# Local transformer in a chain of blocks: the mask into the scores' banks by ScalarE, the state transposed once and spread through DRAM, a step's scores ahead of its weighted state

## The chip, the cores and the metric

The kernel runs on one core of one Trainium2 chip. Its engines work side by side, each through its own queue in order: TensorE (PE, with the weight loads as PEld), VectorE (DVE), ScalarE (ACT), GpSimd (POOL), and SyncE (SP), which issues the DMAs. They wait for each other through semaphores. The metric is device microseconds of one execution; several executions are made and their median is taken.

## The reference

Two blocks follow each other, each an attention and a feed-forward part with modulated layer norms, on x of 16 batch rows, 256 positions, 128 channels. What the change touches is the second part of the first block, a local transformer of 6 layers:

```
for i in range(6):
    x = attn_layer(shift_tokens(x), Wqkv[i], q_scale[i], k_scale[i], Wo[i]) + x
    x = ffn_layer(shift_tokens(x), ...) + x

def attn_layer(x, Wqkv, qs, ksc, Wo):         # 16 heads of 64
    q, k, v = heads of x @ Wqkv
    q = l2norm(q) * qs;  k = l2norm(k) * ksc
    q = q * cos * scale + rotate_half(q) * sin * scale
    k = k * cos / scale + rotate_half(k) * sin / scale
    # windows of 32 queries, each on 64 keys: its own window and the one before
    sim = q_window @ k_two_windows.T * 8
    sim = where(mask, -max, sim)              # i < j or i > j + 32 or no key
    out = softmax(sim) @ v_two_windows
    return out @ Wo
```

Everything is float32.

## The kernel before, in words

The local transformer keeps its state in eight SBUF tiles `zs[u]`, one for each unit u of two batch rows, channels on the partitions, with 32 columns of zeros ahead of the 256 positions (PAD), so that a window's 64 keys are 64 neighbouring columns. The values are not projected: the weights of value and output are merged once a layer (`merge_vo`), so that a head's output is its weighted state (probabilities times the state's rows) times a merged matrix.

One loop (L1050) runs over 192 steps: 6 layers x 8 units x 4 steps, where a step handles two pairs of heads of one unit. It is a pipeline written out by hand: pass n of the loop issues, in this order, work of several steps:

- `scaled` (L792, L795): POOL multiplies the keys of step n-4 by their inverse norms, which come spread over the partitions in tiles `kn`; two pairs, so two instructions.
- `merging` (L924, L927): PE multiplies the weighted state of step n-9 by the merged matrices into the bank `y`.
- parts of earlier units' feed-forward (`ffn`, L948), handed out piece by piece by `go_on`.
- `rotate` (L712, L714): POOL adds the rotated halves `got` to queries and keys of step n-1, four instructions.
- `flipped` (L884, L888): PE turns the probabilities of step n-5, in two halves, into `prT`.
- `windows` (L797): twice in four steps, for one batch row each, PE transposes eight windows of 64 columns of the state (L805), DVE and ACT copy them to `xw`, and a DMA copies partitions 0 to 63 of `xw` to 64 to 127 (L813), so that the two heads of a pair find the rows on their own half of the array.
- `masked` (L816, L821): PE writes the mask into the two banks of the scores by an identity matmul, from a bf16 tile; the scores are then accumulated on it.
- `norms_sum` (L717) in even passes: PE sums squares of two steps.
- `weighted` (L898, L906): for step n-8, two rounds of eight matmuls, each round into two banks, which ACT (L921) and DVE (L919) copy to `zx`.
- `scores` (L832, L843): 128 small matmuls for step n-4, half of them on the keys of each pair, into two banks; then `maxima` (L852) on DVE: a maximum (L855) and its scaled negative `nb` (L857) for each bank.
- `norms_inverse` (L734) in even passes, and parts of `ffn`.
- `project` (L685) of step n, for two pairs of heads: each time two products of weights and state on PE (L698), and for each the square on ACT (L701) and two products with rotary tables on DVE (L703 into `sent`, L706 into q or k). Four DMAs then exchange halves of `sent` into `got` (L708, L709). Ahead of each square stands a quarter of `exponentials` (L860, L865) of the first pair of step n-4: two ACT instructions of 64 columns.
- the rest: `divided` (L876: a reciprocal on DVE, L878, and a product on POOL, L880) of the first pair, the exponentials of the second pair, and its `divided`.
- `widened` (L781, L786): four DMAs that spread the inverse norms of step n-3 from DRAM into two tiles `kn`.

On PE, DVE, ACT and POOL this program order is the order of the queues. The order of SP's DMAs is made by the scheduling layer. PSUM has eight banks here: four that rotate for all products (`bank()`, L58), three for scores (`sim`), one for `y`. The temporaries of `work` rotate through eleven buffers of 128x512, `kn`, `got` and `sent` through two each.

Of the kernel before, what the change touches and what calls it, by code (L numbers as in the profile page):

```python
# [10 lines left out]
F32 = mybir.dt.float32  # L11
# [7 lines left out]
B, L, D = 16, 256, 128  # L19
NU = B // 2  # L20
# [24 lines left out]
def adaln_kernel(  # L45
# [12 lines left out]
    def bank():  # L58
        return stage["ps"].tile([128, 512], F32, tag="mm", name="mm")
# [20 lines left out]
    def small(tag, shape, bufs=4):  # L80
        return (stage.get("small") or sm).tile(list(shape), F32, tag=tag, name=tag, bufs=bufs)
# [518 lines left out]
    with ExitStack() as es:  # L600
# [23 lines left out]
        nc.sync.dma_start(sel, io["c_sel"])  # L624

        ks = [persistent(f"k{j}", (128, 2, PAD + L)) for j in range(8)]
        rope = lc.tile([128, 2, 2, L], F32, tag="rope", name="rope")
        nc.sync.dma_start(rope, io["c_rope"].rearrange("p (j a) t -> p j a t", j=2))

# [164 lines left out]
            k = ks[m % 8][:, :, PAD:]  # L794
            nc.gpsimd.tensor_tensor(k, k, two(kn), ALU.mult)  # L795

        def windows(u, s):  # L797


            xw = atile("xw", (128, 8, 128))  # L800
            for g in range(2):
                pt = bank()
                for j in range(4):
                    w0 = 32 * (4 * g + j)
                    nc.tensor.transpose(  # L805
                        pt[0:64, j * 128 : (j + 1) * 128], zs[u][:, s, w0 : w0 + 64], ident
                    )
                dst = xw[0:64, 4 * g : 4 * g + 4, :].rearrange("p w d -> p (w d)")
                if g:
                    nc.vector.tensor_copy(dst, pt[0:64, :])  # L810
                else:
                    nc.scalar.copy(dst, pt[0:64, :])
            nc.sync.dma_start(xw[64:128], xw[0:64])  # L813
            return xw

        def masked():  # L816

            sims = []
            for par in range(2):
                sim = pss.tile([128, 512], F32, tag="sim", name="sim")  # L820
                nc.tensor.matmul(  # L821
                    sim,
                    ident16,
                    maskb.unsqueeze(1).to_broadcast([128, 2, 256]),
                    start=True,
                    stop=False,
                    skip_group_check=True,
                )
                sims.append(sim)
            return sims  # L830

        def scores(sims, m, qs):  # L832

# [42 lines left out]
        def divided(pr, ssum):  # L876
            rsum = small("rsum", (128, 8))
            nc.vector.reciprocal(rsum, ssum.rearrange("p t h -> p (t h)"))  # L878
            prf = pr.rearrange("p t h k -> p (t h) k")
            nc.gpsimd.tensor_tensor(  # L880
                prf, prf, rsum.unsqueeze(2).to_broadcast([128, 8, 64]), ALU.mult
            )

        def flipped(p, x, pr, prT):  # L884

            pt = bank()
            for st in range(4):
                nc.tensor.transpose(  # L888
                    pt[:, st * 128 : (st + 1) * 128],
                    pr[:, x, st].rearrange("p h k -> p (h k)"),  # L890
                    ident,
                )
            if x:
                nc.vector.tensor_copy(prT[:, p + x, :], pt)
            else:
                nc.scalar.copy(prT[:, p + x, :], pt)

        def weighted(j, xw, prT):  # L898

            zx = atile("zx", (128, 2, NP, 128))  # L900
            for k in (2 * j, 2 * j + 1):
                pz = [bank(), bank()]
                for w in range(2):
                    for par in range(2):
                        r = slice(64 * par, 64 * par + 64)
                        nc.tensor.matmul(  # L906
                            pz[par][:, w * 256 : (w + 1) * 256],
                            xw[r, (2 * k + w) % 8, :],
                            prT[r, :, 64 * k + 32 * w : 64 * k + 32 * w + 32],
                            start=True,  # L910
                            stop=True,
                            skip_group_check=True,
                        )
                for par in range(2):
                    c0 = 64 * (k % 2)
                    dst = zx[:, par, :, c0 : c0 + 64].rearrange("p a (w q) -> p w a q", w=2)
                    src = pz[par].rearrange("p (w a q) -> p w a q", w=2, a=NP)
                    if par:
                        nc.vector.tensor_copy(dst, src)  # L919
                    else:  # L920
                        nc.scalar.copy(dst, src)  # L921
            return zx

        def merging(j, zx, vo, py):  # L924
# [125 lines left out]
        while n < N + 9 or behind:  # L1050
# [26 lines left out]
            for s, lag in ((0, 7), (1, 9)):  # L1077
                v, r = divmod(n - lag, QS)
                if r == 0 and 0 <= v < DEPTH * NU:
                    xws[v, s] = windows(v % NU, s)  # L1080
            sims = masked() if 0 <= n - 4 < N else None
            if 0 <= n - 5 < N:
                flipped(p, 1, prs.pop(n - 5), prTs[i, u])

            if n % 2 == 0 and 2 <= n <= N:
                n2 = norms_sum([squares.pop(m) for m in range(2 * n - 4, 2 * n)])
            v, r = divmod(n - 8, QS)
            if 0 <= v < DEPTH * NU:
# [32 lines left out]
            if layer + 1 < DEPTH:  # L1121
# [476 lines left out]
```

## Time and profile before

| | us |
|---|---|
| median of three runs | 4208.1 (4206.4 to 4209.5) |
| the profiled execution, its own time | 4207.8 |
| its span, first to last instruction | 4206.0 |
| the layer loop, by the rows of its scores (L843) | about 303 to 3572 |
| a unit of four steps, 2006.49 to 2074.08 | 67.59 |

Mean granted clock of TensorE over the span: 0.981. In the layer loop each step's rows repeat with small differences, so that one unit of four steps, read engine by engine, tells most of the loop. In the profile's rows the first numbers are a start and a length in us, or, in groups, the busy time and the mean length in ns of one instruction and then the idle time ahead of them and what ended it. "SPq" is the queue of DMA issues. The shares of the span are averages: which wait ends last is read from the rows of a step.

### The profile page before, as it was taken

Reading aid. Unit: us, or ns where it says so; the run is one execution under the profiler, and the core shown is the slowest. Engines: PE = TensorE matmul, PEld = TensorE weight load, DVE = VectorE, ACT = ScalarE, POOL = GpSimd, SP = SyncE. Lnnn points to the kernel's source line nnn. Section 1 sums busy time; section 2 is a strip of 40 time slices with the busy share of each in tenths; the row PEclk is TensorE's granted clock in tenths of the full one; section 3 lists DMA queues with packets and bytes.
Section 4 is the critical chain, followed back from the end, with each engine's and each line's share of the span. In section 5 each row is a group of like instructions: output and inputs, shape, how many; then the busy total and the mean of one; then the engine's idle time right before and its main releaser. Section 6 shows DMA issues by size and latency. Waiting matters only on the chain.

```text
span 4206.0 us, 118202 instructions
## 1 busy us (share of the span) xinstructions
PE 3938.9 (94%) x45491; PEld 2580.1 (61%) x45491; DVE 2856.0 (68%) x6005; ACT 2753.1 (65%) x9640; POOL 2655.1 (63%) x3374
## 2 busy tenths in 40 slices
PE   7877999999999999999999999999999999799998
PEld 4534666666666666666666666666666666455554
DVE  6746767677767767676777777776767675476664
ACT  4535666667666666667666667666666766276665
POOL 5446666776666676666676766767666665155453
PEclk9878999999999999999999999999999999899999
DMA  1333444444444444444444444444434442200000
GB/s 41 41 90 97 106 109 105 109 107 105 106 105 114 104 110 105 105 110 102 111 109 105 112 103 106 108 110 105 110 100 105 104 105 72 64 1 6 9 3 11
DMA packets 193547, 371.06 MB, mean 88 GB/s; under 512 B 42537, under 2 KB 83416, under 8 KB 192984
## 3 DMA queue, kind: packets, MB, share of 16 engines
q1 hardware_dynamic: 192984, 363.50, 34.3%
q8 instruction: 360, 5.90, 0.6%
q14 instruction: 203, 1.66, 0.1%
HBM read 127.92 MB, written 8.91 MB: 33 GB/s over the span
## 4 chain that ended last, share of the span: by engine, by line
PE 46%; DVE 22%; ACT 19%; issue 7%; POOL 5%; DMA 1%; SPq 0%; POOLq 0%; DVEq 0%; ACTq 0%
ACT pr L865 11%; PE mm L906 9%; PE sim L843 7%; DVE sent L703 6%; ACT sq L701 4%; PE mm L722 4%; PE mm L888 4%; POOL pr L880 4%; DVE k L706 3%; DVE q L706 3%; PE mm L698 3%; DVE mx L855 3%; PE mm L805 2%; PE mm L1376 2%; PE sim L1303 2%
## 5 line engine op out<-in xcount | busy, mean ns | idle before, releaser
L865 ACT ACTIVATE pr<-sim,nb,rq 128x64 f32<-128x64 f32 x3072 | 1229.5, 454 | 336.8 <-DVE nb L857 318.3
L880 POOL TENSOR_TENSOR pr<-pr,rsum 128x512 f32<-128x512 f32 x384 | 398.3, 1042 | 807.3 <-DVE rsum L878 761.8
L865 ACT ACTIVATION_READ_ACCUMULATOR pr<-sim,nb,rq 128x1 f32 x3072 | 784.5, 255 | 0.0
L927 PEld LDWEIGHTS y<-zx,wvo 128*128 128x128 f32 x6144 | 716.1, 192 | 92.1 <-issue 89.0
L927 PE MATMUL y<-zx,wvo 128*128 128x128 f32 x6144 | 717.7, 275 | 1.3 <-ACT zx L921 1.2
L698 PE MATMUL mm<-z,wqk 128*128 128x512 f32 x1536 | 706.9, 602 | 8.6 <-DMA wqk<-in_L_ffn_Wqkv_dram 6.7
L703 DVE SCALAR_TENSOR_TENSOR sent<-mm,vec,rope 128x512 f32<-128x512 f32 x768 | 570.4, 743 | 118.2 <-ACT sq L701 110.2
L714 POOL TENSOR_TENSOR q<-q,got 128x512 f32<-128x512 f32 x384 | 488.3, 1272 | 12.7 <-DMA got<-sent 10.2
L714 POOL TENSOR_TENSOR k<-k,got 128x512 f32<-128x512 f32 x384 | 496.2, 1292 | 0.0
L795 POOL TENSOR_TENSOR k<-k,kn 128x512 f32<-128x512 f32 x384 | 481.9, 1274 | 17.9 <-DMA kn<-rkh 17.9
L701 ACT ACTIVATE sq<-mm 128x512 f32<-128x512 f32 x768 | 475.7, 619 | 23.3 <-PE mm L698 23.3
L698 PEld LDWEIGHTS mm<-z,wqk 128*128 128x128 f32 x1536 | 278.7, 192 | 322.9 <-issue 234.7
L919 DVE COPY zx<-mm 128x512 f32<-128x512 f32 x384 | 265.6, 692 | 262.0 <-PE mm L906 262.0
L921 ACT COPY zx<-mm 128x512 f32<-128x512 f32 x384 | 224.9, 586 | 287.0 <-PE mm L906 287.0
L906 PE MATMUL mm<-prT,xw 64*128 64x256 f32 x3072 | 389.7, 391 | 3.8 <-DVE zx L919 2.0
L855 DVE TENSOR_REDUCE mx<-sim 128x8 f32<-128x512 f32 x384 | 263.1, 685 | 171.9 <-PE sim L843 171.9
L906 PEld LDWEIGHTS mm<-prT,xw 64*128 64x128 f32 x3072 | 293.5, 187 | 121.7 <-issue 92.2
L1346 POOL TENSOR_TENSOR pr<-pr,rsum 128x256 f32<-128x256 f32 (+1 forms) x256 | 205.1, 832 | 241.7 <-DVE rsum L1344 218.3
L888 PE MATMUL mm<-ident,pr 128*128 128x128 f32 x1536 | 244.6, 282 | 105.1 <-POOL pr L880 75.9
L888 PEld LDWEIGHTS mm<-ident,pr 128*128 128x128 f32 x1536 | 174.9, 142 | 270.0 <-POOL pr L880 240.6
L843 PEld LDWEIGHTS sim<-k,q 64*32 64x32 f32 x24576 | 265.8, 105 | 83.3 <-issue 55.2
L843 PE MATMUL sim<-k,q 64*32 64x64 f32 x24576 | 299.7, 226 | 15.9 <-POOL k L795 8.1
(253 smaller groups left out, 6461.5 us busy)
## 6 DMA issues: line engine op xcount, KB each, us to landing
got<-sent SPq DMA_DIRECT2D x1536, 128.0 KB
kn<-rkh SPq DMA_DIRECT2D x768, 128.0 KB
xw<-xw SPq DMA_DIRECT2D x96, 256.0 KB
wqk<-in_L_ffn_Wqkv_dram SPq DMA_DIRECT2D x48, 128.0 KB
bhome<-brow SPq DMA_DIRECT2D x1, 3072.0 KB
wv<-in_L_ffn_Wqkv_dram SPq DMA_DIRECT2D x12, 256.0 KB
wo<-in_L_ffn_Wo_dram SPq DMA_DIRECT2D x12, 256.0 KB
xt<-in_x_dram SPq DMA_DIRECT2D x8, 256.0 KB
```

The source lines that it names most:

```text
L698: nc.tensor.matmul(pp, wqk[:, j, :], xs, start=True, stop=True)
L701: nc.scalar.activation(sq, pp, AF.Square)
L703: nc.vector.scalar_tensor_tensor(two(sent[:, j, :]), two(pp), scale, tab[1], ALU.mult, ALU.mult)
L714: nc.gpsimd.tensor_tensor(r, r, two(got[:, j, :]), ALU.add)
L795: nc.gpsimd.tensor_tensor(k, k, two(kn), ALU.mult)
L843: nc.tensor.matmul(sims[par][32 * c : 32 * c + 32, c0 : c0 + 64], q[r, s, t0 : t0 + 32], k[r, s, t0 : t0 + 64], start=False, stop=True, sk ...
L855: nc.vector.tensor_reduce(mx, sim.rearrange("p (b k) -> p b k", b=8), AX.X, ALU.max)
L865: nc.scalar.activation(pr[:, x, st, par, :], sims[par][:, b * 64 : (b + 1) * 64], AF.Exp, bias=nbs[par][:, b : b + 1], scale=rn[:, par, b ...
L880: nc.gpsimd.tensor_tensor(prf, prf, rsum.unsqueeze(2).to_broadcast([128, 8, 64]), ALU.mult)
L888: nc.tensor.transpose(pt[:, st * 128 : (st + 1) * 128], pr[:, x, st].rearrange("p h k -> p (h k)"), ident,)
L906: nc.tensor.matmul(pz[par][:, w * 256 : (w + 1) * 256], xw[r, (2 * k + w) % 8, :], prT[r, :, 64 * k + 32 * w : 64 * k + 32 * w + 32], star ...
L927: nc.tensor.matmul(py[:, j * 128 : (j + 1) * 128], vo[:, h, :], zx[:, h % 2, h // 2, :], start=(h == 0), stop=(h == 2 * NP - 1), skip_grou ...
```

## The change

There are four edits, all in the local transformer.

1. The state is transposed once a unit (`upright`, new): four transposes of 128 columns into one bank, one ACT copy to `xt`, two DMAs that store it row by row into a DRAM tile `rows` (two of them, used in turn, each with 32 zero rows ahead). `windows` then no longer uses PE, DVE or ACT: four DMAs load 32 partitions each of `xw` from the DRAM rows, for either half.
2. `masked` fills one bank a call instead of two, and is called twice a pass, for the step after the one whose scores are made in this pass: once behind `flipped`, once at the end. After the first three banks it is an ACT copy from the bf16 mask to the bank; the first three are still matmuls.
3. `scores` and `maxima` of step n-4 stand ahead of `weighted` of step n-8.
4. Exponentials and division are one sequence (`softmax`): its first quarter is issued between the two rounds of `weighted`, the next ones ahead of the squares of `project` (so the first pair's division comes ahead of the last square), the rest at the end.

```diff
+        rows = [dr.tile([2, PAD + L, D], F32, tag=f"rows{j}", name=f"rows{j}") for j in range(2)]
...
-        def windows(u, s):
+        def upright(u, home):
+
+            pt = bank()
+            for t in range(4):
+                s, c = t // 2, PAD + 128 * (t % 2)
+                nc.tensor.transpose(
+                    pt[:, t * 128 : (t + 1) * 128], zs[u][:, s, c : c + 128], ident
+                )
+            xt = work("xt").rearrange("p (s h d) -> p s h d", s=2, h=2)
+            nc.scalar.copy(xt.rearrange("p s h d -> p (s h d)"), pt)
+            for s in range(2):
+                nc.sync.dma_start(
+                    home[s, PAD : PAD + L, :].rearrange("(h p) d -> p h d", p=128), xt[:, s]
+                )
+
+        def windows(s, home):
             xw = atile("xw", (128, 8, 128))
...
-            nc.sync.dma_start(xw[64:128], xw[0:64])
+            for r in range(0, 128, WIN):
+                t0 = r % (2 * WIN)
+                nc.sync.dma_start(
+                    xw[r : r + WIN],
+                    home[s, t0 : t0 + L, :].rearrange("(w p) d -> p w d", p=WIN),
+                )
             return xw
+        banks = []
         def masked():
...
+            if len(banks) < 3:
+                nc.tensor.matmul(
+                    sim, ident16, src, start=True, stop=False, skip_group_check=True
+                )
+            else:
+                nc.scalar.copy(sim.rearrange("p (x c) -> p x c", x=2), src)
+            banks.append(sim)
...
+        def softmax(*args):
+
+            for x in range(2):
+                yield from exponentials(x, *args)
+                pr, ssum = args[-2:]
+                divided(pr[:, x], ssum[:, x])
...
-        def weighted(j, xw, prT):
+        def weighted(j, xw, prT, between):
...
+                if k % 2 == 0:
+                    next(between, None)
             return zx
...
-                    xws[v, s] = windows(v % NU, s)
-            sims = masked() if 0 <= n - 4 < N else None
+                    if s == 0:
+                        upright(v % NU, rows[v % 2])
+                    xws[v, s] = windows(s, rows[v % 2])
             if 0 <= n - 5 < N:
                 flipped(p, 1, prs.pop(n - 5), prTs[i, u])
+            if 0 <= n - 3 < N:
+                masked()
+            sims = banks[2 * (n - 4) : 2 * (n - 3)] if 0 <= n - 4 < N else None
...
-            v, r = divmod(n - 8, QS)
-            if 0 <= v < DEPTH * NU:
-                zxs[v, r] = weighted(r, xws[v, r // 2], prTs[v // NU, v % NU])
-            go_on(behind)
             if sims:
...
                 nbs = [maxima(sims[par], rn[:, par]) for par in range(2)]
                 ssum = small("ssum", (128, 2, 4, 2))
+                between = softmax(sims, nbs, rn, pr, ssum)
+            else:
+                between = iter(())
+            v, r = divmod(n - 8, QS)
+            if 0 <= v < DEPTH * NU:
+                zxs[v, r] = weighted(r, xws[v, r // 2], prTs[v // NU, v % NU], between)
+            go_on(behind)
...
-            between = exponentials(0, sims, nbs, rn, pr, ssum) if sims else iter(())
...
             if sims:
-                for x in range(2):
-                    for _ in between:
-                        pass
-                    divided(pr[:, x], ssum[:, x])
-                    between = exponentials(1, sims, nbs, rn, pr, ssum) if x == 0 else iter(())
+                for _ in between:
+                    pass
                 prs[n - 4] = pr
             if 0 <= n - 3 < N:
+                masked()
```

More of the change, by code (lines that the diff above doesn't have):

```diff
@@ L626, in adaln_kernel @@
         ks = [persistent(f"k{j}", (128, 2, PAD + L)) for j in range(8)]
+        rows = [dr.tile([2, PAD + L, D], F32, tag=f"rows{j}", name=f"rows{j}") for j in range(2)]
+        zero = work("zero")[0:PAD, 0:D]
+        nc.vector.memset(zero, 0.0)
+        for home in rows:
+            for s in range(2):
+                nc.sync.dma_start(home[s, 0:PAD, :], zero)
         rope = lc.tile([128, 2, 2, L], F32, tag="rope", name="rope")
@@ L795, in scaled @@
             nc.gpsimd.tensor_tensor(k, k, two(kn), ALU.mult)
-        def windows(u, s):
-            xw = atile("xw", (128, 8, 128))
[L801 to L812, printed above, removed]
-            nc.sync.dma_start(xw[64:128], xw[0:64])
+        def upright(u, home):
[7 more added lines that the diff above has]
+            nc.scalar.copy(xt.rearrange("p s h d -> p (s h d)"), pt)
+            for s in range(2):
+                nc.sync.dma_start(
+                    home[s, PAD : PAD + L, :].rearrange("(h p) d -> p h d", p=128), xt[:, s]
+                )
@@ L814, in windows @@
+        def windows(s, home):
+            xw = atile("xw", (128, 8, 128))
+            for r in range(0, 128, WIN):
[4 more added lines that the diff above has]
+                )
             return xw
+        banks = []
         def masked():
-            sims = []
-            for par in range(2):
-                sim = pss.tile([128, 512], F32, tag="sim", name="sim")
+            sim = pss.tile([128, 512], F32, tag="sim", name="sim")
+            src = maskb.unsqueeze(1).to_broadcast([128, 2, 256])
+            if len(banks) < 3:
@@ L821, in masked @@
                 nc.tensor.matmul(
[L822 to L827, printed above, removed]
-                )
-                sims.append(sim)
-            return sims
+                    sim, ident16, src, start=True, stop=False, skip_group_check=True
+                )
+            else:
+                nc.scalar.copy(sim.rearrange("p (x c) -> p x c", x=2), src)
```

## The prediction

> **What bounds the kernel now.** The sum is made against the profiled execution, 4207.8 us: a span of 4206.0 and 1.8 around it. The median of the three runs, 4208.1, is 0.3 away. I read the page first (busy shares, chain), then the stretches between two blocks of scores, then one step engine by engine, then the places where a load came late.
>
> ```profile
> PE 3938.9 (94%) x45491; PEld 2580.1 (61%) x45491; DVE 2856.0 (68%) x6005; ACT 2753.1 (65%) x9640; POOL 2655.1 (63%) x3374
> ...
> PE 46%; DVE 22%; ACT 19%; issue 7%; POOL 5%; DMA 1%; SPq 0%; POOLq 0%; DVEq 0%; ACTq 0%
> ```
>
> TensorE (PE) is nearly always busy, but only 46% of the chain lies on it. The layer loop has 192 steps, four to a unit. The stretches of one unit, cut where a block of scores (L843) ends (columns: length, then busy PE, PEld, DVE, ACT, POOL, then clock):
>
> ```profile
> 2006.49:2023.27 16.78, 16.55 (x218) 10.60 (x218) 12.75 (x21) 10.58 (x40) 10.35 (x9) 1.00 0.43 114
> 2023.27:2039.26 15.99, 15.21 (x219) 11.81 (x219) 11.57 (x22) 11.01 (x42) 11.50 (x22) 1.00 0.42 102
> 2039.26:2056.65 17.39, 17.13 (x222) 10.60 (x222) 11.16 (x19) 13.58 (x44) 12.98 (x11) 1.00 0.41 107
> 2056.65:2074.08 17.43, 16.66 (x215) 11.14 (x214) 12.76 (x23) 11.88 (x42) 12.25 (x22) 1.00 0.41 99
> ```
>
> I call them I to IV: 67.59 us a unit, 48 units. The end of I, by the timelines of PE, POOL and the DMA queue:
>
> ```profile
> 2017.38 0.66 PE L888 MATMUL mm<-ident,pr 128*128 128x128 f32 x4 [0.23 <-POOL pr L880]
> 2017.97 1.92 PE L722 MATMUL mm<-sq,sel 128*32 128x512 f32 x16
> 2019.86 2.00 PE L906 MATMUL mm<-prT,xw 64*128 64x256 f32 x16
> 2021.79 1.48 PE L843 MATMUL sim<-k,q 64*32 64x64 f32 x128
> ```
> ```profile
> 2016.29 1.04 POOL L880 TENSOR_TENSOR pr<-pr,rsum 128x512 f32<-128x512 f32 x1 [0.47 <-DVE rsum L878]
> 2017.29 2.52 POOL L795 TENSOR_TENSOR k<-k,kn 128x512 f32<-128x512 f32 x2
> ```
> ```profile
> 2015.72 0.59 SPq L709 DMA_DIRECT2D got<-sent  x1
> 2018.59 2.41 SPq L786 DMA_DIRECT2D kn<-rkh  x4
> ```
>
> PE waits only for the division (L880). POOL's two scalings of k (L795) end at 2019.81, and the scores need them at 2021.79, because the weighted state (L906) stands between: 2 us of slack. The kn loads go out after the eight got loads, and 13 to 17 us ahead of the scaling that uses them. A third thing is seen on DVE, beside POOL's row (third line):
>
> ```profile
> 2006.52 0.69 DVE L855 TENSOR_REDUCE mx<-sim 128x8 f32<-128x512 f32 x1 [0.78 <-PE sim L843]
> 2007.24 0.37 DVE L857 SCALAR_TENSOR_TENSOR nb<-mx,rq 128x8 f32<-128x8 f32 x1
> ```
> ```profile
> 2006.33 1.25 POOL L714 TENSOR_TENSOR q<-q,got 128x512 f32<-128x512 f32 x1
> ```
>
> The small nb row takes 0.17 alone, but here it ends 0.03 after POOL's row does: it sits out POOL's instruction. Last, one of the six steps where a kn load stood behind the got loads:
>
> ```profile
> 2219.09 0.59 SPq L709 DMA_DIRECT2D got<-sent  x1
> 2219.73 5.51 SPq L786 DMA_DIRECT2D kn<-rkh  x5
> ```
> ```profile
> 2220.10 1.30 POOL L795 TENSOR_TENSOR k<-k,kn 128x512 f32<-128x512 f32 x1
> 2222.75 1.28 POOL L795 TENSOR_TENSOR k<-k,kn 128x512 f32<-128x512 f32 x1 [1.35 <-DMA kn<-rkh]
> ```
>
> The scaling starts 3.0 us after the issue (2.9 to 3.8 over the six) and POOL stands 1.35 us; the slack hides it, that step took 16.9.
>
> **The change part by part.** *Taken from PE.* The two mask matmuls move PE on by 0.43 us (2016.55 at full pace; the next starts at 2034.77 + 0.43 in II). The sixteen transposes of a unit cost 0.87 and 1.03, the four that replace them as much as a flip, 0.45. That is 4 x 0.43 + 1.90 - 0.45 = 3.2 us a unit. The waits of PE for the division sum to 1.8 a unit. Alone: -5.0 x 48 = -240.
>
> *Masks on ScalarE.* Two copies of 128x512; no row writes a bank from SBUF. Bounds: 0.24 (L776, the smallest copy) and 0.59 (L921); 0.59, as it has that shape. One stands behind the step's last exponential, while reciprocal, division and scaling run (0.2 + 1.04 + 2.5); the other while PE sums norms. Cost 0; without cover 1.18 x 192 = 226.
>
> *Spread through DRAM.* Ten DMAs for two a unit, at 0.6 issue each. The first load waits for the stores: at most 3.8 us twice by the late loads above, plus 3.6 issue, against a whole step until it is used. Cost 0 on PE. DMA share 0.42 leaves room for the bytes, +0.75 MB on 7 a unit.
>
> *Scores ahead of the weighted state.* Clock: T is the end of a block of scores. Scalings now stand directly before the scores' second half (0.85 to T), and POOL's four rotations follow until T+4.27, with borders at T+0.43, 1.71, 2.99. DVE does maxima first: mx to 0.72, nb to 1.73 (border), mx to 2.44, nb to 3.02, and only then its zx copies, to 3.73 and 4.42; before, they stood ahead of the maxima. PE takes banks from a ring of four, and the second bank wanted after the weighted state (1.96 long) is the one this first copy empties. So PE waits at T+3.8: I, project's second product, 0.95; II, the state's mean (L953), 1.4; III, project's first, 1.7 (POOL has L972 and L974 ahead of the rotations, borders 0.4 later); IV, project's first, 1.4. PE's path: I 16.78 - 0.43 - 0.40 + 0.95 = 16.9. III 17.39 - 0.35 - 0.65 + 1.7 = 18.1. IV 17.43 less masks, windows and waits (2.4), + 1.4 = 16.4.
>
> ACT's chain: zx copies (0.48 pace) and two pairs of exponentials (0.77) stand before the first square. In II that square waits for the product behind the late mean: T+5.65, before T+2.37. From there to the last exponential it was 7.98; one pair is done already: 12.9. Reciprocal and division to 14.3, scalings to 16.85, scores: **II 17.65**. IV, with its table load (1.28) now between copy and exponentials: last exponential 11.9, division 13.25, scaling 15.8, **16.6**.
>
> *What the DMA queue does.* SP's own order moves too. As the changed program is built, in the steps before even ones (those that end I and III) 184 of the 192 loads of the second kn tile stand behind the eight got loads, before 10; of the first tile 46, before 2. In order on one queue, they wait for got, and got for the fourth `sent` of project. I: first square T+3.9, `sent` rows from 4.55 at 0.66 each, with a reciprocal: fourth ends 9.5; four got issues to 12.0; kn at 12.0, 12.55, 13.15; plus 3.0: scalings 15.0 and 16.3 to 17.55; + 0.85: **I 18.4** (PE's 16.9 is shorter). III: L980 and L981 on DVE (0.68 + 0.85) come before `sent`: fourth ends 11.25, got 13.75, kn 14.3, landed 17.3, scaled 18.6: **III 19.45**. The slack that hid this is gone, since scores no longer stand behind the weighted state.
>
> Sum: 18.4 + 17.65 + 19.45 + 16.6 = 72.1, +4.5 a unit, x 48 = +216: 4207.8 + 216 = 4424. Ends from the kn delay (2.9 to 3.8): 4414 to 4500 (two steps x 0.8 x 48).
>
> [...] The clock: with PE's waits in II and III there may be dips. The trace shows one behind waits of 2.02 and 1.84 us near the loop's end:
>
> ```profile
> 3582.70:3589.50 6.80, 6.04 (x20) 4.38 (x21) 2.12 (x4) 1.17 (x2) 0.00 (x0) 0.50 0.01 2
> ```
>
> In it the weighted state took 3.88 for 2.00. One such dip a unit costs at most half of 6.8: +163. [...]
>
> **The rivals.** *A: kn lands in time after all* (0.20). Then I is 16.9 and III 18.1, the bank wait and ACT's chain alone decide: 69.25, +80: 4288. For it: before, kn needed 3 us of a lead of 13 to 17. Against: the order as built.
>
> *B: faster* (0.14). If DVE's copy doesn't hold PE's bank (the nb rows don't meet POOL, as in 102 of 339 in the trace) and kn is in time, the first square of II isn't late: I 16.0, II 15.5, III 16.4, IV 16.4: 64.3, -158: 4050. It decides where the kn wait at POOL stays under 0.5 us and the bank wait under 0.3.
>
> *C: dips* (0.13): 4424 + 163 = 4587. For it: with 86% busy (65.5 less the 3.2 taken, of 72.1), PE is between the loop's 97% at clock 1.00 and its tail.
>
> *D: no change* (0.03), where A's loss meets B's gain.
>
> **How the numbers follow.** Forecast 0.50: 4424. Below it A and B, above it C. The range from 4220 to 4600 leaves out B and part of D; below A's 4288 I go by half the bank waits (5.45 x 48 / 2 is 131, of which about half lies on the path, so 4288 - 66). The forecast's own range is 4340 to 4510. A measurement of this kernel can tell about 0.2% from no change. Faster 0.15 (B and a part of D), same 0.03, slower 0.82.
>
> **What would show it.** Right: in the groups, POOL's scaling of k idle for DMA kn, in all 200 us or more (before 17.9); scores idle for POOL k; PE or PEld of project and mean idle for the DVE zx copy; stretches of about 18, 18, 19, 17; no mask and fewer transposes on PE. Wrong: if POOL's scaling still waits 20 us in all, I and III are too long here; if project doesn't wait for zx, II and IV too. What would make it wrong at the root: `sent` early enough that got and kn go out sooner, or nb that doesn't wait for POOL.

## The result, and the profile after

The changed kernel takes 4391 us at the median (4386 to 4394), the kernel before 4208: the ratio is 1.043, with a 95% interval from 1.042 to 1.045. That is 183 us more; the forecast was 216 more. The profiled execution has a span of 4389.3 us.

The page of the changed kernel, busy shares and chain:

```profile
PE 3884.4 (88%) x44534; PEld 2548.8 (58%) x44534; DVE 2870.8 (65%) x5910; ACT 2900.3 (66%) x9973; POOL 2655.2 (60%) x3374
...
PE 27%; DVE 23%; issue 11%; POOL 11%; ACT 10%; DMA 9%; SPq 8%; POOLq 0%; DVEq 0%; ACTq 0%
```

TensorE (PE) was busy 3939 us before and is busy 3884 now, and its share of the chain fell from 46% to 27%. What is new on the chain is DMA (9%, before 1%) and SP's queue (8%, before 0%). One unit of four steps, cut at the ends of the scores (columns as in the forecast: length, busy PE, PEld, DVE, ACT, POOL, clock):

```profile
1955.83:1974.12 18.29, 16.80 (x216) 10.56 (x215) 12.97 (x21) 11.46 (x42) 9.54 (x9) 1.00 0.60 150
1974.12:1991.53 17.41, 14.48 (x209) 10.77 (x209) 11.27 (x21) 11.46 (x43) 13.23 (x22) 1.00 0.46 114
1991.53:2010.56 19.03, 16.92 (x220) 10.68 (x220) 11.95 (x19) 14.59 (x46) 11.06 (x11) 1.00 0.36 96
2010.56:2027.03 16.47, 15.43 (x210) 10.82 (x209) 12.58 (x22) 12.72 (x44) 13.24 (x22) 1.00 0.38 91
```

PE's work in the unit came down from 65.55 to 63.63 us, and the unit got longer, 71.2 for 67.6. Over the units of the loop, its first and last ones left out, the medians of I to IV are 18.96, 17.73, 18.96 and 16.48 (forecast 18.4, 17.65, 19.45, 16.6).

The end of I, first SP's queue, then POOL:

```profile
1962.30 0.53 SPq L715 DMA_DIRECT2D got<-sent  x1
...
1966.81 0.59 SPq L716 DMA_DIRECT2D got<-sent  x1
1967.44 1.88 SPq L793 DMA_DIRECT2D kn<-rkh  x3
```
```profile
1966.54 1.04 POOL L895 TENSOR_TENSOR pr<-pr,rsum 128x512 f32<-128x512 f32 x1 [1.02 <-DMA got<-sent]
1970.38 1.27 POOL L802 TENSOR_TENSOR k<-k,kn 128x512 f32<-128x512 f32 x1 [2.79 <-DMA kn<-rkh]
```

Three of the four kn loads go out at 1967.44, behind the last got load. The scaling starts 2.9 us later, and POOL stood 2.79 us for it. In the kernel before, the scaling came 14 us behind its last load's issue at the median. In all, the groups of POOL's scaling, PE's projection, and the mask copies read:

```profile
L705 PE MATMUL mm<-z,wqk 128*128 128x512 f32 x1536 | 721.7, 609 | 95.9 <-DVE zx L941 87.0 <-DMA wqk<-in_L_ffn_Wqkv_dram 7.7 <-ACT wvT L678 0.7
...
L802 POOL TENSOR_TENSOR k<-k,kn 128x512 f32<-128x512 f32 x384 | 484.3, 1272 | 298.3 <-DMA kn<-rkh 288.9 <-DMA xw<-rows 6.3 <-DMA wqk<-in_L_ffn_Wqkv_dram 1.1
...
L844 ACT CAST sim<-maskb 128x512 f32<-128x512 bf16 x381 | 245.4, 644 | 0.0
```

and POOL's scaling in the kernel before:

```profile
L795 POOL TENSOR_TENSOR k<-k,kn 128x512 f32<-128x512 f32 x384 | 481.9, 1274 | 17.9 <-DMA kn<-rkh 17.9
```

POOL's wait for kn is 288.9 us in all (before 17.9), and PE's projection waits 87 us for DVE's zx copy. A mask copy takes 0.64 us, a little above the 0.59 that bounded it. The small nb rows on DVE, in II, and POOL's rows beside them:

```profile
1974.22 0.69 DVE L870 TENSOR_REDUCE mx<-sim 128x8 f32<-128x512 f32 x1 [3.67 <-PE sim L858]
1974.95 0.74 DVE L872 SCALAR_TENSOR_TENSOR nb<-mx,rq 128x8 f32<-128x8 f32 x1
1975.61 0.68 DVE L870 TENSOR_REDUCE mx<-sim 128x8 f32<-128x512 f32 x1
1976.32 0.59 DVE L872 SCALAR_TENSOR_TENSOR nb<-mx,rq 128x8 f32<-128x8 f32 x1
1976.83 1.27 DVE L941 COPY zx<-mm 128x512 f32<-128x512 f32 x2
```
```profile
1974.38 1.28 POOL L721 TENSOR_TENSOR k<-k,got 128x512 f32<-128x512 f32 x1
1975.61 1.27 POOL L721 TENSOR_TENSOR q<-q,got 128x512 f32<-128x512 f32 x1
```

Each nb ends 0.03 us after a row of POOL's rotations does (1975.66 and 1976.88). This is no chance: of the 384 nb rows of this run 377 last longer than 0.2 us, and every one of them ends 0.02 to 0.04 us after a row of POOL's (before: 241, all of them too). Only then come the zx copies, as the forecast had it.

### The profile page after: what moved, and what is told of

Its sections match the earlier page's. It is cut to its first block, busy times and chain, and to the rows that moved or that the text cites. A ratio compares the mean times of both kernels' runs of the same rounds, so it can differ in the third digit from the quotient of the medians.

```text
span 4389.3 us, 117277 instructions
## 1 busy us (share of the span) xinstructions
PE 3884.4 (88%) x44534; PEld 2548.8 (58%) x44534; DVE 2870.8 (65%) x5910; ACT 2900.3 (66%) x9973; POOL 2655.2 (60%) x3374
## 4 chain that ended last, share of the span: by engine, by line
PE 27%; DVE 23%; issue 11%; POOL 11%; ACT 10%; DMA 9%; SPq 8%; POOLq 0%; DVEq 0%; ACTq 0%
POOL k L802 7%; DVE sent L710 6%; DMA kn<-rkh 4%; PE sim L858 4%; ACT pr L880 4%; DVE q L713 4%; PE mm L705 3%; DVE mx L870 3%; PE mm L928 3%; SPq L793 3%; SPq L716 2%; SPq L715 2%; DMA xw<-rows 2%; POOL pr L895 2%; DVE zx L941 2%
## 5 line engine op out<-in xcount | busy, mean ns | idle before, releaser
L880 ACT ACTIVATE pr<-sim,nb,rq 128x64 f32<-128x64 f32 x3072 | 1240.9, 447 | 19.3 <-DVE nb L872 15.4
L705 PE MATMUL mm<-z,wqk 128*128 128x512 f32 x1536 | 721.7, 609 | 95.9 <-DVE zx L941 87.0
L880 ACT ACTIVATION_READ_ACCUMULATOR pr<-sim,nb,rq 128x1 f32 x3072 | 758.6, 247 | 0.0
L802 POOL TENSOR_TENSOR k<-k,kn 128x512 f32<-128x512 f32 x384 | 484.3, 1272 | 298.3 <-DMA kn<-rkh 288.9
L858 PE MATMUL sim<-k,q 64*32 64x64 f32 x24576 | 352.5, 239 | 166.6 <-POOL k L802 153.7
L858 PEld LDWEIGHTS sim<-k,q 64*32 64x32 f32 x24576 | 284.4, 112 | 303.2 <-POOL k L802 242.4
L928 PE MATMUL mm<-prT,xw 64*128 64x256 f32 x3072 | 437.5, 423 | 13.9 <-DVE zx L941 9.8
L928 PEld LDWEIGHTS mm<-prT,xw 64*128 64x128 f32 x3072 | 324.7, 208 | 70.0 <-issue 13.3
L916 DVE COPY prT<-mm 128x512 f32<-128x512 f32 x192 | 132.7, 691 | 263.5 <-PE mm L910 262.2
L1360 ACT ACTIVATE pr<-lg,nm 128x128 f32<-128x128 f32 (+1 forms) x512 | 226.3, 443 | 116.7 <-DVE nm L1349 95.1
L910 PE MATMUL mm<-ident,pr 128*128 128x128 f32 x1536 | 233.9, 281 | 78.0 <-POOL pr L895 67.2
```

The costliest lines, as they stand in the source:

```text
L705: nc.tensor.matmul(pp, wqk[:, j, :], xs, start=True, stop=True)
L858: nc.tensor.matmul(sims[par][32 * c : 32 * c + 32, c0 : c0 + 64], q[r, s, t0 : t0 + 32], k[r, s, t0 : t0 + 64], start=False, stop=True, sk ...
L880: nc.scalar.activation(pr[:, x, st, par, :], sims[par][:, b * 64 : (b + 1) * 64], AF.Exp, bias=nbs[par][:, b : b + 1], scale=rn[:, par, b ...
L910: nc.tensor.transpose(pt[:, st * 128 : (st + 1) * 128], pr[:, x, st].rearrange("p h k -> p (h k)"), ident,)
L928: nc.tensor.matmul(pz[par][:, w * 256 : (w + 1) * 256], xw[r, (2 * k + w) % 8, :], prT[r, :, 64 * k + 32 * w : 64 * k + 32 * w + 32], star ...
```

## The experiments

All times are medians against the kernel before, which stood at 4207 to 4209 us beside each of them. The step lengths I to IV are medians over the loop, worked out from the ends of the scores in each trace.

### The order on SP's queue: kn_early

```diff
+            if 0 <= n - 3 < N:
+                for m in (2 * (n - 3), 2 * (n - 3) + 1):
+                    kns[m] = widened(m, home)
             for m in (2 * n, 2 * n + 1):
                 if n < N:
...
             if 0 <= n - 3 < N:
                 masked()
-                for m in (2 * (n - 3), 2 * (n - 3) + 1):
-                    kns[m] = widened(m, home)
```

> The changed kernel with the calls that load kn placed ahead of the projection, so that on SP's queue the loads of both tiles stand ahead of the step's got loads (16 of 192 behind them in the steps before even ones, not 184). Nothing else moves. Theory (the order on the queue makes I and III long): POOL's scaling of k waits under 80 us in all for kn (289 now), I comes to about 16.9 and III to about 18.1 (18.7 and 18.9 now), so about 2.6 us a unit x 48 = 125 us less: 4391 to about 4266. Rival (the late loads lie beside the wait for the bank and ACT's chain, which hold I and III by themselves): the wait at POOL goes, but the time stays within 30 us: 4360 or more.

Measured: 4264 us (ratio 1.013, 1.011 to 1.015), 127 less than the changed kernel. The group of POOL's scaling in it:

```profile
L802 POOL TENSOR_TENSOR k<-k,kn 128x512 f32<-128x512 f32 x384 | 482.2, 1276 | 10.5 <-DMA kn<-rkh 10.4
```

The wait fell from 288.9 to 10.4 us. I is 16.67 and III 18.04 (expected 16.9 and 18.1), II 17.43 is 0.3 shorter, IV 16.47 stayed. Only the place of four loads on a queue was changed, so this shows that, in the changed kernel, the order of the loads costs 127 of the 183 us. The other 56 remain.

### DVE's nb rows: one_nb, and both edits: kn_early_one_nb

```diff
-            mx = small("mx", (128, 8))
-            nc.vector.tensor_reduce(mx, sim.rearrange("p (b k) -> p b k", b=8), AX.X, ALU.max)
-            nb = small("nb", (128, 8))
+            mx = small("mx", (128, 2, 8))
+            for par in range(2):
+                nc.vector.tensor_reduce(
+                    mx[:, par], sims[par].rearrange("p (b k) -> p b k", b=8), AX.X, ALU.max
+                )
+            nb = small("nb", (128, 2, 8))
             nc.vector.scalar_tensor_tensor(nb, mx, -1.0, rn, ALU.mult, ALU.mult)
-            return nb
+            return [nb[:, par] for par in range(2)]
...
```

> The changed kernel with both maxima first and one instruction for both nb rows, so that DVE sits out one POOL instruction in a step and not two before it copies the zx bank. The kn loads stay behind got. Theory (DVE's nb rows hold the bank that PE wants next): PE's waits for the DVE zx copy (87 + 157 + 27 us) fall under a third, the first copy ends about 1.3 us earlier; II falls by about 1.2, IV by about 0.4, and sent, got and kn in I and III come about 1 us earlier: about 3.5 x 48 = 170 less, 4391 to about 4220. Rival (the wait for the bank is covered, ACT's chain is set by the exponentials and not by the late product): within 30 us of 4391.

Measured: 4354 us (1.035, 1.033 to 1.036), 37 less than the changed kernel and not 170. The wait of PE's projection for DVE in it:

```profile
L705 PE MATMUL mm<-z,wqk 128*128 128x512 f32 x1536 | 703.6, 601 | 11.5 <-DMA wqk<-in_L_ffn_Wqkv_dram 7.7 <-DVE zx L944 1.6 <-ACT wvT L678 0.7
```

So the nb rows did hold the bank: 87.0 us of PE's wait became 1.6. II fell by 1.07, as expected. But I (18.89), III (18.82) and IV (16.47) did not move by more than 0.14. The expectation that `sent`, got and kn would come 1 us earlier there was wrong. In I the first square starts 3.69 us into the step in both kernels, and the fourth `sent` ends at 9.1 in both. In III the first `sent` does come 0.8 us earlier in 18 of 44 units, and the median of these steps is 18.16. In 21 of the others a feed-forward row on DVE ahead of it (L1008, 0.5 to 0.9 us long in those 18) lasts 1.1 to 1.7 us and ends 0.28 to 0.29 us after a row of POOL's; the fourth `sent` then ends at 10.28, as before (10.30), and these steps take 18.92. The kn loads wait for that fourth one.

> Both edits together. Theory: I 16.0 (16.9 less the wait for the bank of 0.95), II 16.4, III 16.7, IV 16.1: 65.2 a unit against 71.75, x 48 = 314 less: 4391 to about 4077, below the kernel before. Rival (dips of the granted clock, 0.963 over the span, belong to the new order itself): they stay and the time is some 100 us higher, 4180, no faster than 1% below before. Rival (ACT's or POOL's chain is the next bound): above 4200.

Measured: 4219 us (1.003, 1.002 to 1.004), 172 less than the changed kernel, 46 less than kn_early, and still not below before. I to IV are 16.12, 16.80, 17.67, 17.11, in all 67.7, where 65.2 was expected. POOL waits 12.6 us for kn, and in the projection PE's matmuls wait 16 us for the bank (59 in kn_early; its weight loads another 56, in kn_early 124), so little is left of the two waits of the forecast, and the 3.2 us a unit taken from PE should show. They don't. What closes a step now is seen in its II, by POOL's rows and then by the chain:

```profile
1968.18 1.04 POOL L898 TENSOR_TENSOR pr<-pr,rsum 128x512 f32<-128x512 f32 x1 [1.13 <-DVE ve L997]
```
```profile
1969.18 2.52 POOL k L802 x2
1971.70 0.04 issue
1971.74 1.19 PE sim L858 x61
```

The scores wait for the scalings of k, and these stand behind the last division. IV closes in the same way; in the III of the same unit the chain runs through `sent`, got and the scaling. Whether work taken from PE can show in such a loop is the subject of the next runs.

### The three edits one by one: order_of_before, masks_only, spread_only, reorder_only

In the first, the weighted state stands ahead of the scores again:

```diff
+            v, r = divmod(n - 8, QS)
+            if 0 <= v < DEPTH * NU:
+                zxs[v, r] = weighted(r, xws[v, r // 2], prTs[v // NU, v % NU], iter(()))
+            go_on(behind)
             if sims:
                 m = 2 * (n - 4)
...
-                between = softmax(sims, nbs, rn, pr, ssum)
-            else:
-                between = iter(())
-            v, r = divmod(n - 8, QS)
-            if 0 <= v < DEPTH * NU:
-                zxs[v, r] = weighted(r, xws[v, r // 2], prTs[v // NU, v % NU], between)
-            go_on(behind)
...
```

> The changed kernel with the weighted state ahead of the scores again and the exponentials placed as before: masks on ScalarE and the spread through DRAM remain. Theory (both are hidden, only the new order costs): PE loses the masks and twelve of sixteen transposes, 3.2 us a unit x 48 = 153 less than before: 4055, and up to 25 more where the second kn tile is still late (98 of 192 loads behind got, with 2 us of slack). Rival (the masks on ScalarE, 0.64 us each, or the traffic of the spread are what costs): no faster than before, 4208 or more.

Measured: 4249 us (1.010, 1.009 to 1.012). The theory asked for 4055 to 4080; the rival had it, slower than before. POOL waits 123 us for kn in it. The other three start from the kernel before and take over one edit of the change each; their diffs are those parts of the change's own diff.

> The kernel before, with only the masks moved from PE to ScalarE, at the places where the changed kernel has them. Theory of the forecast (the copies are hidden): 0.43 us a step less on PE, x 192 = 83: 4208 to about 4125. Rival, from the run with the old order, which was 41 us slower than before although PE had 3.2 us a unit less to do (two copies of 0.64 us lie on ScalarE's path from the maxima to the last exponential): up to 1.29 x 192 = 247 less 83, so between 4208 and 4372.

Measured: 4218 us (1.003, 1.001 to 1.004). Neither the 83 us gained nor a large loss.

> The kernel before, with only the state's transposes and the spread through DRAM changed. Theory of the forecast (hidden): 1.45 us a unit less on PE, x 48 = 70: 4208 to about 4138. Rival (the eight or ten more DMAs on SP push kn behind got: on SP's queue 98 of the 192 second tiles stand there now, 10 before): 98 x (3.0 - 2.0 us of slack) = 98 more, less 70: about 4236. If masks_only and spread_only together make about 41 more than before, the two explain the run with the old order.

Measured: 4227 us (1.005, 1.004 to 1.007). POOL waits 111.8 us for kn in it.

> The kernel before, with only the new order of the step (scores and softmax ahead of the weighted state); masks and eight window transposes of each half remain on PE. On SP's queue 59 of the second kn tiles stand behind got (10 before, 184 in the changed kernel). Theory (the new order costs by the bank wait and by DVE, and where kn is late): I 17.4, II 17.0, III 18.5, IV 17.4 and 59 late loads x 2 us: about 70.3 + 2.5 = 72.8 a unit against 68.4, at most +210: 4330 to 4420. Rival (the new order by itself takes away the waits for the division and costs nothing where kn is in time): 1.8 x 48 = 86 less, 4122.

Measured: 4275 us (1.016, 1.015 to 1.018), 55 below the low end of the theory's range, and 153 above the rival. I to IV are 16.55, 17.21, 18.42, 17.08; POOL waits 111.7 us for kn, PE 104.2 us for the bank in the projection.

The edits cost 10, 20 and 67 us one by one (against 4207 beside them), 97 in sum, and 183 together. On SP's queue 12, 98 and 59 of the 192 loads of second kn tiles (of the steps before even ones) stand behind got in them, and 184 in the changed kernel. The remaining 86 us are thus what the edits do to one another, and kn_early shows that the queue's order is worth more than that.

### Does PE bind the kernel before? no_masks, and spread_kn_early

```diff
-                nc.tensor.matmul(
-                    sim,
-                    ident16,
-                    maskb.unsqueeze(1).to_broadcast([128, 2, 256]),
-                    start=True,
-                    stop=False,
-                    skip_group_check=True,
-                )
...
                                 k[r, s, t0 : t0 + 64],
-                                start=False,
+                                start=True,
```

> The kernel before without any masks: the two mask matmuls of a step are left out and each scores matmul writes its place afresh, so keys outside the window count in the maxima and the sums. Nothing goes to ScalarE in their place. Theory (PE binds the kernel before; the masks cost 0.43 us a step there): 83 us less, 4208 to 4125, and masks_only (4218) then shows that the copies cost 93 on ScalarE. Rival (the step is closed by maxima, exponentials, division, transposes and scores; PE's work ahead of the division is not on it): no less than 4190, and the copies in masks_only cost under 30.

Measured: 4207 us (1.0003, 0.9993 to 1.0012). PE lost 60 us of work and the time did not move at all. The chain of one step of it, in order of time (columns: start, length, what):

```profile
1938.74 0.88 ACT pr L857 x4
...
1945.50 0.12 DVE rsum L870
...
1947.29 1.05 POOL pr L872
1948.35 0.04 issue
1948.39 0.66 PE mm L880 x4
1949.05 1.85 PE mm L722 x16
1950.90 1.97 PE mm L898 x16
1952.87 1.45 PE sim L835 x91
1954.33 0.68 DVE mx L847
```

This is a loop: maxima, exponentials and projections, reciprocal, POOL's second division, the second set of transposes (L880), the sums of norms, the weighted state, the scores, and the next maxima. The masks stand on PE ahead of the second set of transposes, which waits for the division whatever PE did before it. In this step PE stands 0.86 us there; in the step of the kernel before that the forecast shows, with the masks, 0.23. Over the whole run PE stands longer ahead of these transposes. Their matmuls and weight loads, in the kernel before and then without masks:

```profile
L888 PE MATMUL mm<-ident,pr 128*128 128x128 f32 x1536 | 244.6, 282 | 105.1 <-POOL pr L880 75.9 <-ACT rkT L776 17.6 <-DVE z L942 5.3
L888 PEld LDWEIGHTS mm<-ident,pr 128*128 128x128 f32 x1536 | 174.9, 142 | 270.0 <-POOL pr L880 240.6 <-POOL k L795 7.6 <-issue 5.4
```
```profile
L880 PE MATMUL mm<-ident,pr 128*128 128x128 f32 x1536 | 251.4, 287 | 152.3 <-POOL pr L872 100.6 <-ACT fg L983 23.9 <-ACT rkT L776 17.5
L880 PEld LDWEIGHTS mm<-ident,pr 128*128 128x128 f32 x1536 | 167.2, 143 | 294.0 <-POOL pr L872 282.2 <-POOL k L795 5.6 <-issue 3.5
```

The matmuls' idle time ahead of them grew from 105.1 to 152.3 us, which is 47 of the 60 us that PE lost in work. So PE's 94% busy time did not make PE the bound. It also follows that the mask copies cost about 10 us on ScalarE (masks_only less no_masks), so the forecast's price of nothing was nearly right, and it was the saving that did not exist.

```diff
+            if 0 <= n - 3 < N:
+                for m in (2 * (n - 3), 2 * (n - 3) + 1):
+                    kns[m] = widened(m, home)
             between = exponentials(0, sims, nbs, rn, pr, ssum) if sims else iter(())
```

(and the same three lines taken out behind the projection, in spread_only)

> spread_only (4227) with the calls that load kn placed ahead of the projection: 8 of 384 tiles behind got in the steps before even ones, 142 in spread_only. Theory (the spread costs nothing on PE; it costs because its ten DMAs push kn behind got): POOL's wait for kn falls from 112 to about 20 and the 70 us of transposes come out: 4227 to about 4140. Rival (the step is closed by the division, PE's savings are waited for there, and kn behind got was mostly covered by the 2 us of slack): between 4200 and 4227. Rival (the bytes of the spread slow the other loads): unchanged, 4227, with POOL still waiting.

Measured: 4215 us (1.002, 1.001 to 1.003). POOL's wait for kn is gone, 2.2 us in all, and with it 13 us of time, but the 70 us of transposes again bring nothing: they too stand on PE between the two sets of transposes of the softmax, ahead of the wait. PE was busy 30 us less than in the kernel before, and its matmuls stand 32 us longer ahead of the softmax's transposes (137.3 for 105.1). If all of the saving is waited for, the traffic of the spread costs at most the 7 us that are left against the kernel before.

### Opening the loop: scale_ahead_flip_behind, flips_on_scalar, masks_back_on_pe

kn_early and one_nb stay in. The scalings for the next step go ahead of POOL's last division, and the softmax's transposes go behind the scores, so that the scores no longer wait for the division:

```diff
-            if 0 <= n - 4 < N:
-                for m in (2 * (n - 4), 2 * (n - 4) + 1):
-                    scaled(m, kns.pop(m))
...
+            if 0 <= n - 5 < N:
+                i, u, p = place(n - 5)
+                if p == 0:
+                    prTs[i, u] = atile("prT", (128, NP, 512))
+                flipped(p, 0, prs[n - 5], prTs[i, u])
+            if 0 <= n - 5 < N:
+                flipped(p, 1, prs.pop(n - 5), prTs[i, u])
             v, r = divmod(n - 8, QS)
             if 0 <= v < DEPTH * NU:
...
+            if 0 <= n - 3 < N:
+                for m in (2 * (n - 3), 2 * (n - 3) + 1):
+                    scaled(m, kns.pop(m))
             if sims:
                 for _ in between:
```

(the calls of `flipped` ahead of the scores go away)

> kn_early_one_nb, and the next step's scalings of k put on POOL ahead of the step's last division, and the transposes of the softmax (L913) put on PE behind the scores and ahead of the weighted state. Theory (the step's loop is the chain maxima, exponentials, last division, scalings, scores, which the scores need not wait for): PE is then the bound, 62.4 us a unit of work and about 1 of waits: 63.5 against 68.85, x 48 = 257 less than 4219: about 3962. Rival (ScalarE's own work between maxima and last exponential is the bound, whatever follows it): within 1% of 4219. Rival (the half-speed stretches of the clock set it): no lower than 4100.

Measured: 4215 us (1.002, 1.001 to 1.003), so no gain. The chain is now 71% on PE, but PE found a new wait. The begin of II in this kernel, PE, then DVE and POOL:

```profile
2161.51 1.09 PE L913 MATMUL mm<-ident,pr 128*128 128x128 f32 x8
2164.81 1.53 PE L931 MATMUL mm<-prT,xw 64*128 64x256 f32 x11 [2.21 <-issue]
```
```profile
2161.59 1.29 DVE L871 TENSOR_REDUCE mx<-sim 128x8 f32<-128x512 f32 x2 [1.81 <-PE sim L858]
2162.92 1.19 DVE L875 SCALAR_TENSOR_TENSOR nb<-mx,rq 128x16 f32<-128x16 f32 x1
2164.03 0.68 DVE L919 COPY prT<-mm 128x512 f32<-128x512 f32 x1
```
```profile
2162.82 1.25 POOL L721 TENSOR_TENSOR k<-k,got 128x512 f32<-128x512 f32 x1
```

The weighted state of II is the first to use the transposes made just ahead of it, and their copy on DVE stands behind the maxima and the nb row, which again ends 0.04 us after a row of POOL's does (2164.07). The profile calls the 2.21 us "issue"; the copy that ends at 2164.71 shows what it was. The next run puts that copy on ScalarE, which is idle there (3.16 us, from 2162.79 to 2165.94):

```diff
-            if x:
-                nc.vector.tensor_copy(prT[:, p + x, :], pt)
-            else:
-                nc.scalar.copy(prT[:, p + x, :], pt)
+            nc.scalar.copy(prT[:, p + x, :], pt)
```

> scale_ahead_flip_behind (4215) with both copies of the transposed softmax (L917 to L921 there) on ScalarE, which stands idle for nb at that point, and none on DVE, where the copy stood behind maxima and nb. Theory (in II, PE stands 2.2 us and in IV 0.6 us for that copy before the weighted state): II falls from 17.4 to about 15.7, IV by 0.5: 2.2 a unit x 48 = 106 less, about 4110, faster than the kernel before by about 2%. Rival (ScalarE's chain of exponentials grows by 0.6 us and takes it back): within 0.7% of 4215.

Measured: 4046 us, 0.962 of the kernel before (0.961 to 0.963), and 168 less than without this one edit. I to IV are 16.21, 15.97, 16.50, 15.59, 64.3 in all. PE at the same place, and one whole unit by stretches:

```profile
1874.51 1.09 PE L913 MATMUL mm<-ident,pr 128*128 128x128 f32 x8
1876.33 2.07 PE L928 MATMUL mm<-prT,xw 64*128 64x256 f32 x16 [0.73 <-ACT prT L918]
```
```profile
1858.58:1874.58 16.00, 16.00 (x216) 10.23 (x216) 11.88 (x19) 11.88 (x43) 11.04 (x10) 1.00 0.66 163
1874.58:1890.55 15.97, 14.27 (x209) 10.96 (x209) 9.82 (x19) 11.97 (x44) 11.22 (x20) 1.00 0.36 88
1890.55:1907.09 16.54, 16.54 (x220) 10.64 (x220) 10.49 (x17) 14.89 (x47) 13.38 (x13) 1.00 0.60 155
1907.09:1922.66 15.57, 15.54 (x208) 10.73 (x209) 10.78 (x20) 13.29 (x45) 11.10 (x21) 1.00 0.33 77
```

PE has 62.35 us of work in this unit, the 65.55 of before less the 3.2 that the forecast worked out, and I, III and IV are PE's work and nothing else. How much of the 162 us against the kernel before belongs to the change and how much to the opened loop isn't shown, since the loop was not opened in the kernel before; the next run tells it for the masks alone. The gain is larger than the 106 us expected: II fell by 1.54 and IV by 0.77, as expected or a little less and a little more, but I and III fell by 0.5 each as well, for which no run gives the reason.

Last, the masks back on PE in this kernel:

```diff
-            if len(banks) < 3:
-                nc.tensor.matmul(
-                    sim, ident16, src, start=True, stop=False, skip_group_check=True
-                )
-            else:
-                nc.scalar.copy(sim.rearrange("p (x c) -> p x c", x=2), src)
+            nc.tensor.matmul(
+                sim, ident16, src, start=True, stop=False, skip_group_check=True
+            )
...
-            if 0 <= n - 3 < N:
+            if 0 <= n - 4 < N:
+                masked()
                 masked()
...
-            if 0 <= n - 3 < N:
-                masked()
```

> flips_on_scalar (4046) with both masks of a step as matmuls on PE again, ahead of the scores, and none on ScalarE. no_masks showed that in the kernel before the mask matmuls cost nothing. Theory (with the loop through the division opened, PE binds, so the same 0.43 us a step now costs): 83 us more, about 4129. Rival (ScalarE or DVE binds there as well, and 1.29 us a step less on ScalarE pays for it): 4046 or below.

Measured: 4064 us (0.965, 0.964 to 0.967), 18 us more, which neither theory nor rival gave. PE's busy time rose by 40 us. The half-speed stretches of the clock in the loop fell from 96 to 37 us, which may return up to 29 us of PE's time (an estimate: half of the 59). PE's wait ahead of the scores, where the masks stand now, fell too, in flips_on_scalar and then here:

```profile
L858 PE MATMUL sim<-k,q 64*32 64x64 f32 x24576 | 321.6, 229 | 68.6 <-POOL k L802 63.8 <-issue 3.2 <-ACT sim L844 1.3
```
```profile
L855 PE MATMUL sim<-k,q 64*32 64x64 f32 x24576 | 312.3, 227 | 40.6 <-POOL k L802 36.7
```

So some 27 us of the masks' work fill a wait for the scalings of k. ScalarE's busy time fell by 187 us, and what that gives was not tried. The masks' share of the change, in this order of the work, is thus 18 us and not 83.

## Why the prediction was right, point by point

**The kn loads behind got.** Right in place, sign and size. The forecast put the kn issue of I at 12.0 us into the step and the second scaling at 16.3; the trace has 11.7 and 16.67 at the median, and I came out at 18.96 for 18.4. III: 14.3 for the second tile's issue was too late, since the fourth `sent` ends at 10.3 and not at 11.25, and III came out at 18.96 for 19.45. Undone alone, the order gives back 127 us.

**ACT's chain in II and IV.** Right: last exponential of II at 12.69 (forecast 12.9), of IV at 11.73 (11.9); steps 17.73 and 16.48 (17.65 and 16.6).

**The wait for the bank.** The mechanism is right, the size was not. In the unit above PE's matmuls stand 0.86 (II), 1.35 (III) and 0.94 us (IV) for it, and in I the eight products of the projection take 0.27 us longer than in II (3.87 for 3.60): 3.4 in all, where 0.95, 1.4, 1.7 and 1.4 were put down, 5.45 in all. The edit that takes it away, one_nb, is worth 46 us where kn is in time.

**The sum.** The medians of the four steps sum to 72.13, the forecast to 72.1. That they agree so closely is luck: I came out 0.56 longer than forecast and III 0.49 shorter. The time is 33 us lower, because the forecast multiplied a typical unit by 48. The mean unit grew from 68.42 to 72.39, by 3.97 and not 4.5: the steps at the borders of the layers, long already, grew less. That is some 25 of the 33.

**"Alone: -240".** This is the step that failed, the price put on work taken from PE alone, and the sum did not need it, because I to IV were set by other chains. The 3.2 us a unit taken from PE stood ahead of the second set of transposes, where PE waits for the division. no_masks, masks_only and spread_kn_early show that nothing of it was to be had in the old order (0, 10 and 7 us more than before). The 46% of PE in the chain was the sign: a loop through PE, DVE, ScalarE and POOL, in which PE's share lies behind the division.

**Rival A**, kn in time, 4288: kn_early, which is that case, took 4264. **Rival B**, 4050, asked for kn in time and the bank wait under 0.3 us: kn_early_one_nb meets the first (12.6 us over 192 steps) and the second nearly (16 us by the projection's matmuls, 0.08 a step, and 72 us with its weight loads, 0.37 a step) and took 4219. B failed at the same place as the -240: with the two waits mostly gone the steps still close through the division and the scalings. **Rival C**, dips at +163: the dips came (53 stretches in the loop, before 7), as the row of the kernel before had it, and by the comparison below they were nearly free: 23 us of 163. The forecast's own sum has no term for dips, and no run shows that there should be none; what the runs show in its place is the 53 stretches and these 23 us.

## What to carry to other kernels

An engine that is busy 94% of the time need not bind: ask in what place its work stands, and if what is removed lies ahead of a wait that a loop through other engines sets, nothing comes of it (here 0 us of the masks' 60). Where a scheduler sets a queue's order, read the order of the built program; two or three of a step's four loads behind eight others cost 127 us here, and one moved call gave them back. When two waits are gone and the time stays, look for the loop that closes through all engines, and move out of it what its next step doesn't need, here the transposes of the softmax behind the scores. With that, the kernel with the change went from 4.3% above the kernel before to 3.8% below it; how much of the saving is the change's own wasn't tried, except for the masks (18 us).

## What the runs showed of the hardware

**The clock's half-speed stretches.** In the loop of the changed kernel there are 53 of them, at a granted clock of 0.50, 208 us in all (before 7, 44 us). They are 3.41 us long or twice that, and their starts lie a whole number of 3.41 us apart. One of them, with the stretch ahead of it:

```profile
2131.40:2134.81 3.41, 1.71 (x63) 1.24 (x65) 0.92 (x3) 1.78 (x6) 2.85 (x3) 1.00 0.70 161
2134.81:2138.22 3.41, 3.19 (x103) 2.51 (x94) 1.47 (x2) 0.00 (x0) 3.35 (x4) 0.50 0.22 54
2138.22:2141.64 3.42, 3.15 (x20) 1.79 (x17) 3.35 (x7) 2.87 (x11) 3.42 (x4) 1.00 0.09 28
```

Ahead of it PE was busy 1.71 of 3.41 us, and no single wait in it was longer than 1.13. Between 450 and 3650 us of this run 44 such stretches begin, and in the 3.41 us ahead of each PE was busy for at most 0.67 of the time. Some 30 other lengths of 3.41 us, counted in the same steps from start to start, were as little busy and were followed by none, so PE's busy share alone does not tell where a stretch begins, and what brings one on is not shown. What they cost: steps with such a stretch were longer than those of the same kind without by 0.96 us (12 of I), 0.36 (32 of II) and nothing (28 of III), 23 us in all by this comparison of steps, which is no experiment. That other waits cover the rest of the lost pace is likely and not shown. The +163 of rival C took all of it as lost.

**nb beside POOL.** The single nb row of both halves, 128x16, takes 0.38 us at its mean in one_nb and 0.70 in scale_ahead_flip_behind, and at least 0.17. Of its 192 rows 117 and 176 last longer than 0.2 us, and all of these end 0.02 to 0.04 us after a row of POOL's. What decides is where it meets POOL: in the II shown above it starts 0.10 us after a row of POOL's begins and takes 1.19, and in the II shown of flips_on_scalar 0.34 us before one ends (at 1876.36), and takes 0.38:

```profile
1876.02 0.38 DVE L875 SCALAR_TENSOR_TENSOR nb<-mx,rq 128x16 f32<-128x16 f32 x1
```
